# A graph network's first blocks in a new order: block 0 through layer 0 ahead of block 1, its norm on ScalarE, and the setup spread over two passes

## The chip, the cores and the metric

The kernel runs on one core of a Trainium2 chip. A core has five engines that work side by side, each through its own queue in order: TensorE (PE; its weight loads are listed as PEld), VectorE (DVE), ScalarE (ACT), GpSimd (POOL) and SyncE (SP), which here only issues DMA transfers. An engine that meets an instruction whose input isn't there yet waits, and everything behind it in its queue waits too. The metric is the device time of one execution in microseconds; smaller is better.

## The reference

The input x is 128 graphs of 64 nodes with 256 features, and adj is one 64 x 64 adjacency matrix. Four graph layers follow each other, each in the form x = layernorm(x + layer(x)).

```python
# layer 0: attention over adj
Wh = einsum('bnf,fo->bno', x, W)
e = leaky_relu((Wh @ a1)[:, :, None] + (Wh @ a2)[:, None, :], 0.2)
h0 = softmax(where(adj == 0, -inf, e)) @ Wh
# layer 1: attention over 512 edges (src, dst), four heads
e = (leaky_relu(Xq[:, src] + Xq[:, dst], 0.2) * a).sum(-1) + log(adj[src, dst] + 1e-8)
h1 = segment_softmax_and_sum(e, src, Xv[:, dst]) @ W_out.T
# layer 2: (D^-1/2 (adj + I) D^-1/2) x, linear, batchnorm, relu, linear, batchnorm
deg = A.sum(0) + A.sum(1) - diagonal(A)          # A = adj + I
# layer 3: two adjacency layers, then LSTMs over windows of 1, 2, 3 and 4 nodes
```

All of it is float32. Layers 0 and 1 are what the change touches; layers 2 and 3 take most of the time and stay as they are.

## The kernel before

**Blocks.** The 8192 rows of x are cut into 16 blocks (NQ) of 512 rows: 128 partitions by PQ = 4 columns of 256 features, 2 graphs in the partitions of each column. Each block goes through layers 0 and 1 in small steps, which are functions:

- `l0_a` gets the block transposed (block 0 by PE, L231; the others by DVE's transpose of a copy that was loaded in slices, L247). `l0_b` multiplies by W, in which two further columns hold W a1 and W a2 (PE L257, ACT L259), and spreads the second score over 128 columns (`sb`, ACT L262). `l0_c` transposes these (PE L268), adds both scores and the mask (DVE L271), applies the leaky ReLU (L273) and finds the row maximum (L275).
- `l0_x` takes the exponential: for blocks 0 and 1 in four ACT instructions that also sum (L283), for later blocks by a subtraction on DVE (L286) and one ACT instruction (L287). `l0_d` transposes the result on PE (L301) and copies it out on ACT (`eT`, L303). `l0_e` multiplies by the values (PE L311), adds x (DVE L314), and calls `layernorm`: statistics on DVE (L95, L96), the power -1/2 on POOL (L86), and the scaling on POOL (L100). It ends with `load_x(q + 2)`: one DMA for x and eight for the slices, on SP.
- `l1_t` transposes the normed block (PE L231, ACT L232). `l1_qv` makes queries and values for half a block (PE L338 and L341; the queries are split in two by ACT L348 and DVE L349). `l1_graph` forms the edge sums (z, PE L376) and rectifies them (u, ACT L378), `reduce_heads` sums them over features (PE L367). `l1_softmax`, `l1_sums`, `l1_weights` work on two blocks together; `v_a`, `v_b`, `v_c` apply the attention.

**Order.** The program is written down as a list of such calls, and a scheduler puts each engine's instructions in an order of its own, by which input it expects first; the program order of two calls is therefore only a strong hint, and `tc.issue_after` ties an instruction behind another. First comes a head, written out by hand (L580 to L599):

```python
l0_a(0); setup_l0(); ...; l0_b(0); setup_order(); l0_c(0); l0_x(0)
l0_a(1); setup_ends(); l0_b(1); l0_d(0); setup_gather(); setup_queries()
l0_e(0); l0_c(1); l0_x(1); setup_signs(); l0_d(1)
l1_t(0); l1_qv(0, 0); l1_qv(0, 1)
```

Then a loop runs over 16 passes q with eight places b each. At each place one `l1_graph(q, b)` stands, followed by the steps of the list `between[b]`, which belong to blocks q + 1, q + 2 and earlier ones, each tied behind the last PE instruction so far (`step`).

**PSUM.** Nearly all steps take their banks from one ring of three (`bank`, name "m"). A step's first matmul has to wait until the bank's user three places before has been read, by ACT or DVE.

**Setup.** The edges have to be sorted, looked up and counted once. `setup_order`, `setup_ends`, `setup_gather` sort them with comparisons and one-hot matmuls (PE L547, L552; DVE L539 to L559; `gath_r` is what `l1_graph` needs). The rest stands in the list `setup`, from which the loop takes one entry at each place: `setup_zero` (clears two tables by POOL and DMA), `setup_segments` (segment borders, DVE L621 to L624), `setup_bias` (the term log(adj[src, dst] + 1e-8): matmul L655, DVE L657, matmul L659, logarithm on ACT L660), `setup_pairs` (DVE L628 to L634), four times `setup_count` (each three comparisons of 128 x 512 with a sum, DVE L638), `setup_place` (small DVE instructions, L642 to L650) and `setup_adjacency` (degrees of adj + I, scales, and two 128 x 128 matrices for layer 2: DVE L665 to L683, PE L672, L679, L682, POOL L675). Most of these don't depend on the loop, and the scheduler placed many of them into the head: DVE ran L638 from 39 to 50 us.

Of the kernel before, what the change touches and what calls it, by code (L numbers as in the profile page):

```python
# [41 lines left out]
def kernel(ctx: ExitStack, tc: tile.TileContext, i, out):  # L42
# [45 lines left out]
    def layernorm(dst, src, n, engine):  # L88

        st = small.tile([P, n, 6], F32, name="ln_st", bufs=5)  # L90
        mv = small.tile([P, n, 2], F32, name="ln_mv", bufs=5)
        both = small.tile([P, 2, n], F32, name="ln_rs", bufs=5)
        rs, ng = both[:, 0, :], both[:, 1, :]
        for r in range(n):
            nc.vector.bn_stats(st[:, r, :], src[:, r, :])  # L95
            nc.vector.bn_aggr(mv[:, r, :], st[:, r, :])  # L96
        rsqrt(rs, mv[:, :, 1], n)
        nc.vector.tensor_scalar_mul(ng, mv[:, :, 0], -1.0)  # L98
        for r in range(n):
            engine.tensor_scalar(dst[:, r, :], src[:, r, :], ng[:, r:r + 1], rs[:, r:r + 1],  # L100
                                 op0=OP.add, op1=OP.mult)

# [27 lines left out]
    with ExitStack() as two:  # L130
# [147 lines left out]
        def l0_x(q):  # L278
            e, mx = L0[q]["e"], L0[q]["mx"]
            sm = small.tile([P, PQ], F32, name="sm")  # L280
            if q < 2:
                for c in range(PQ):
                    nc.scalar.activation(e[:, c, :], e[:, c, :], AF.Exp, bias=mx[:, c:c + 1],  # L283
                                         accum_out=sm[:, c:c + 1])
            else:
                nc.vector.tensor_add(e, e, mx[:, :, None].to_broadcast([P, PQ, P]))  # L286
                nc.scalar.activation(e, e, AF.Exp)  # L287
            L0[q]["sm"] = sm

        def l0_d(q):  # L290
            e, sm = L0[q]["e"], L0[q]["sm"]
            ri = L0[q]["ri"] = small.tile([P, PQ], F32, name="ri")
            if q < 2:
                nc.vector.reciprocal(ri, sm)
# [10 lines left out]
        def l0_e(q):  # L305
            x, wh, eT, ri = (L0[q][n] for n in ("x", "wh", "eT", "ri"))
            for c2 in range(2):
# [263 lines left out]
        def setup_signs():  # L571
# [4 lines left out]
            for h in range(HEADS):  # L576
                r, c0 = slice((h % 2) * 64, (h % 2 + 1) * 64), CG - HEADS + h
                nc.vector.tensor_copy(apad[r, h // 2, c0:c0 + 1], acol[r, h // 2:h // 2 + 1])

        l0_a(0)  # L580
        setup_l0()
# [15 lines left out]
        l0_d(1)  # L597
        l1_t(0)
        l1_qv(0, 0)  # L599
        l1_qv(0, 1)  # L600


# [48 lines left out]

        def setup_bias():

            pa = bank([E])
            nc.tensor.matmul(pa[:N, :], bd[:N, :N], ohT[:N, 0, :], start=True, stop=True)  # L655
            sel = su.tile([N, E], F32, name="sel")
            nc.vector.tensor_mul(sel, pa[:N, :], ohT[:N, 1, :])  # L657
            pl = bank([E])
            nc.tensor.matmul(pl, ones[:N, :], sel, start=True, stop=True)  # L659
            nc.scalar.activation(lb, pl, AF.Ln, bias=eps8)  # L660

        def setup_adjacency():

            an = su.tile([P, P], F32, name="an")
            nc.vector.tensor_add(an, bd, ident)  # L665
            deg = su.tile([P, 4], F32, name="deg")
# [9 lines left out]
            dd = su.tile([P, P], F32, name="dd")  # L676
            nc.vector.tensor_scalar_mul(dd, ident, deg[:, 3:4])
            ph_ = bank([P])
            nc.tensor.matmul(ph_, an, dd, start=True, stop=True)  # L679
            nc.vector.tensor_scalar_mul(aht, ph_, deg[:, 3:4])  # L680
            pt = bank([P])
            nc.tensor.transpose(pt, bd, ident)  # L682
            nc.vector.tensor_copy(bdT, pt)  # L683
# [22 lines left out]

        def behind(do, q):
            if q < NQ:
                with tc.issue_after([t for t in nc.cur_bb.bb.instructions
                                     if t.engine == mybir.EngineType.Activation][-1]):  # L710
                    do(q)
# [1308 lines left out]
```

## Time and profile before

| what | us |
|---|---|
| median of 3 runs | 2028.21 (2027.94 to 2029.69) |
| the profiled execution, its own time | 2025.54 |
| span of the profiled execution | 2023.8 |
| PE busy in the span | 1934.4 |
| DVE busy | 1277.3 |
| ACT busy | 951.1 |
| POOL busy | 881.1 |
| first matmul | 5.30 |
| first `z` matmul of the loop (L376) | 51.13 |

The page of a profile gives busy time by engine, and the same in 40 slices of 50.6 us as tenths. A row of the timeline gives start, length, engine, line, operation, output and input, the number of instructions merged, and in brackets how long the engine had been idle before it and whose result ended that. In the view of waits a row names the waiting instruction, the one that released it, and the sum, number and longest of these waits in microseconds. The row of windows gives for each stretch of time the busy time of the engines, the TensorE clock that was granted (1.00 is full), and the share of the DMA engines' time in use.

### The profile page before, as it was taken

The page shows a single profiled execution, that of the slowest core. Times are in us where ns is not written, and L with a number is a line of the kernel's source. Part 1 is how long each engine was busy: PE and PEld are TensorE (multiplying, and loading weights), DVE is VectorE, ACT ScalarE, POOL GpSimd, SP SyncE. Part 2 cuts the span into 40 slices and gives each one's busy share as a digit, 9 for nine tenths or more (in the row PEclk, how much of TensorE's full clock was granted, in tenths as well). Part 3 has the DMA queues.
Part 4 walks back from the last instruction along what each step waited for, and adds up shares of the span by engine and source line. Part 5 has one row for each costly group of instructions (what it writes and reads, how often), then busy time and mean ns, then how long its engine had stood idle before and what let it go on. Part 6 is the DMA issues. An engine that isn't in the chain of part 4 may idle for free.

```text
span 2023.8 us, 31384 instructions
## 1 busy us (share of the span) xinstructions
PE 1934.4 (96%) x11447; PEld 1336.6 (66%) x11447; DVE 1277.3 (63%) x2855; ACT 951.1 (47%) x1666; POOL 881.1 (44%) x1020
## 2 busy tenths in 40 slices
PE   5999999998999989899999999999999999999997
PEld 4667777776554445477678577678577668578685
DVE  7567776664556554765566765557865557764566
ACT  2666656665346523644333644343644333543333
POOL 1133343343444632664545544445543445444264
PEclk8999999999999989999999999999999999999998
DMA  5344443332311134432342233133243032131022
GB/s 141 72 68 69 82 79 55 56 56 45 45 46 27 42 132 144 177 125 94 120 141 84 101 124 136 42 130 93 64 146 118 19 115 70 41 120 79 0 63 73
DMA packets 236539, 173.83 MB, mean 86 GB/s; under 512 B 150625, under 2 KB 213601, under 8 KB 233057
## 3 DMA queue, kind: packets, MB, share of 16 engines
q1 hardware_dynamic: 234528, 169.86, 29.6%
q8 instruction: 90, 1.47, 0.3%
q0 software_dynamic: 1024, 1.05, 0.2%
q10 hardware_dynamic: 832, 0.92, 0.1%
q14 instruction: 65, 0.52, 0.1%
HBM read 110.18 MB, written 61.60 MB: 85 GB/s over the span
## 4 chain that ended last, share of the span: by engine, by line
PE 77%; DVE 14%; ACT 4%; issue 2%; POOL 1%; DMA 1%; SPq 0%; DVEq 0%; POOLq 0%; ACTq 0%
PE l L1743 29%; PE l L1699 8%; PE pz L860 4%; PE l L1478 4%; PE m L338 3%; PE pz L789 3%; PE m L257 3%; PE e L367 3%; PE z L376 2%; PE m L461 2%; PE m L341 2%; PE g L1377 2%; PE g L1365 2%; PE pz L1058 2%; DVE cell L1657 1%
## 5 line engine op out<-in xcount | busy, mean ns | idle before, releaser
L1743 PE MATMUL l<-hs,wh 128*128 128x256 f32 (+1 forms) x896 | 276.0, 399 | 3.7 <-DVE hs L1607 3.1
L1743 PE MATMUL l<-xs,wx 128*128 128x256 f32 (+1 forms) x896 | 276.0, 399 | 2.8 <-DVE gate L1762 2.8
L1758 ACT ACTIVATE kept<-l 128x256 f32<-128x256 f32 (+1 forms) x224 | 88.6, 402 | 333.6 <-PE l L1743 332.2
L86 POOL TENSOR_TENSOR ln_rs<-ln_rs,mhalf 128x2 f32<-128x2 f32 (+2 forms) x98 | 85.9, 876 | 344.2 <-DVE ln_rs L98 338.6
L1743 PE MATMUL l<-H,wx 128*128 128x256 f32 (+1 forms) x672 | 210.5, 402 | 4.3 <-DVE gate L1771 3.4
L1743 PE MATMUL l<-hid,wh 128*128 128x256 f32 (+1 forms) x672 | 208.8, 399 | 0.0
L1743 PEld LDWEIGHTS l<-hs,wh 128*128 128x128 f32 x896 | 169.1, 190 | 47.1 <-DVE hs L1607 5.7
L1743 PEld LDWEIGHTS l<-xs,wx 128*128 128x128 f32 x896 | 168.9, 190 | 45.8 <-POOL st L100 2.7
L1699 PE MATMUL l<-H,wx 128*128 128x256 f32 (+5 forms) x672 | 185.0, 431 | 4.9 <-DVE H L116 2.7
L1776 ACT ACTIVATE gate<-gate,bias 128x512 f32<-128x512 f32 (+1 forms) x280 | 170.5, 657 | 40.6 <-DVE gate L1767 34.8
L378 ACT ACTIVATE u<-z 128x1024 f32<-128x1024 f32 x128 | 130.0, 1025 | 71.9 <-PE z L376 71.3
L1699 PEld LDWEIGHTS l<-H,wx 128*128 128x128 f32 x672 | 118.8, 190 | 65.3 <-issue 34.7
L1743 PEld LDWEIGHTS l<-H,wx 128*128 128x128 f32 x672 | 125.7, 190 | 42.6 <-DVE gate L1771 7.4
L1743 PEld LDWEIGHTS l<-hid,wh 128*128 128x128 f32 x672 | 127.2, 190 | 32.0 <-issue 2.9
L1766 POOL TENSOR_TENSOR gate<-gate,kept 128x256 f32<-128x256 f32 (+1 forms) x84 | 65.0, 774 | 145.3 <-DVE kept L1764 145.0
L1771 DVE TENSOR_TENSOR gate<-l,gate 128x256 f32<-128x256 f32 (+1 forms) x112 | 49.9, 446 | 87.6 <-POOL gate L1766 60.8
L349 DVE TENSOR_TENSOR qs<-m,qs 64x256 fp32r<-64x256 f32 x128 | 54.0, 422 | 76.5 <-ACT qs L348 74.4
L1611 POOL TENSOR_TENSOR hs<-hid 128x256 f32<-128x256 f32 (+1 forms) x28 | 26.0, 929 | 171.0 <-DVE hid L1643 87.9
L376 PE MATMUL z<-gath_r,qs 128*128 128x512 f32 x256 | 99.5, 477 | 0.6 <-ACT u L378 0.5
L1665 ACT ACTIVATE gate<-cell 128x512 f32<-128x512 f32 (+1 forms) x88 | 58.6, 666 | 82.6 <-DVE cell L1657 60.6
L1653 POOL TENSOR_TENSOR cell<-gate,cell 128x512 f32<-128x512 f32 (+1 forms) x56 | 75.3, 1366 | 28.2 <-ACT gate L1776 28.2
L1760 DVE TENSOR_TENSOR gate<-l,kept 128x256 f32<-128x256 f32 (+1 forms) x112 | 49.0, 438 | 59.9 <-ACT gate L1776 32.7
(386 smaller groups left out, 4079.4 us busy)
## 6 DMA issues: line engine op xcount, KB each, us to landing
wx<-sums SPq DMA_DIRECT2D x9, 2048.0 KB
wh<-sums SPq DMA_DIRECT2D x9, 1792.0 KB
way<-st SPq DMA_DIRECT2D x54, 256.0 KB
st<-way SPq DMA_DIRECT2D x216, 64.0 KB
xin<-in_x SPq DMA_DIRECT2D x16, 512.0 KB
ld<-table SPq DMA_DIRECT2D x16, 512.0 KB
x_dram<-y SPq DMA_DIRECT2D x16, 512.0 KB
x2r<-x_dram SPq DMA_DIRECT2D x32, 256.0 KB
```

Of the source, the lines that this page charges most:

```text
L86: nc.gpsimd.tensor_tensor(dst, dst, mhalf[:, :n], OP.pow)
L257: nc.tensor.matmul(p_, xT[:, k, c * P:(c + 1) * P], w0[:, k, :], start=k == 0, stop=k == KD - 1)
L376: nc.tensor.matmul(z[:, k, :], L1[q]["qs"][c][:, s, k * P:(k + 1) * P], gath_r, start=True, stop=True)
L378: nc.scalar.activation(u, z, AF.Relu)
L860: nc.tensor.matmul(self.bank[at], lhs, rhs, start=first and n == 0, stop=n == len(self.terms) - 1, skip_group_check=True)
L1478: nc.tensor.matmul(self.bank[at], lhs, rhs, start=new, stop=True, skip_group_check=True)
L1653: nc.gpsimd.tensor_tensor(c, t, c, OP.mult)
L1699: nc.tensor.matmul(b, w.raw[0][:, k, at, m, :], x, start=k == 0, stop=k == KD - 1)
L1743: nc.tensor.matmul(self.banks[j], lhs, rhs, start=src == 0, stop=src == 1)
L1758: nc.scalar.activation(self.keep(j), b, AF.Copy)
L1766: e.tensor_tensor(t[0][:, 1], t[0][:, 1], k[5], OP.add)
L1776: given(lambda: nc.scalar.activation(dst, dst, f, bias=b))
```

## The change

Block 0 goes through the whole of layer 0 before block 1's first matmul, with the lookup's matmul and the logarithm in between. Block 0's norm is scaled by ACT (with one more small DVE product) instead of POOL. Block 1's exponential takes the form of the later blocks, one ACT instruction, and is tied behind ACT's last instruction, after the first half of block 0's queries. Block 1's `l0_e` moves from place (0, 0) of the loop to (0, 1). `setup_adjacency` is cut in three (`setup_degrees`, `setup_scales`, `setup_adjacency`), and the setup list becomes a table of places (q, b); each entry is now tied behind the last PE and the last DVE instruction written before it.

```diff
@@ layernorm
+        if engine is nc.scalar:
+            nc.vector.tensor_mul(ng, ng, rs)
         for r in range(n):
-            engine.tensor_scalar(dst[:, r, :], src[:, r, :], ng[:, r:r + 1], rs[:, r:r + 1],
-                                 op0=OP.add, op1=OP.mult)
+            if engine is nc.scalar:
+                nc.scalar.activation(dst[:, r, :], src[:, r, :], AF.Identity, bias=ng[:, r:r + 1], scale=rs[:, r:r + 1])
+            else:
+                engine.tensor_scalar(dst[:, r, :], src[:, r, :], ng[:, r:r + 1], rs[:, r:r + 1],
+                                     op0=OP.add, op1=OP.mult)
@@ l0_x and l0_d
-            if q < 2:
+            if q == 0:
@@ l0_e
-            layernorm(token_major(q), x, PQ, nc.gpsimd)
+            layernorm(token_major(q), x, PQ, nc.gpsimd if q else nc.scalar)
@@ head
+        def setup_bias():
+            pa = bank([E])
+            nc.tensor.matmul(pa[:N, :], bd[:N, :N], ohT[:N, 0, :], start=True, stop=True)
+            sel = su.tile([N, E], F32, name="sel")
+            nc.vector.tensor_mul(sel, pa[:N, :], ohT[:N, 1, :])
+            around["sel"] = sel
+        def setup_logs():
+            sel = around["sel"]
+            pl = bank([E])
+            nc.tensor.matmul(pl, ones[:N, :], sel, start=True, stop=True)
+            nc.scalar.activation(lb, pl, AF.Ln, bias=eps8)
+        def behind(do, q, engine=mybir.EngineType.Activation):
+            if q < NQ:
+                with tc.issue_after([t for t in nc.cur_bb.bb.instructions if t.engine == engine][-1]):
+                    do(q)
         l0_c(0)
         l0_x(0)
+        setup_ends()
+        setup_gather()
+        setup_bias()
+        l0_d(0)
+        l0_e(0)
+        setup_logs()
         l0_a(1)
-        setup_ends()
         l0_b(1)
-        l0_d(0)
-        setup_gather()
         setup_queries()
-        l0_e(0)
         l0_c(1)
-        l0_x(1)
         setup_signs()
-        l0_d(1)
         l1_t(0)
         l1_qv(0, 0)
+        behind(l0_x, 1)
         l1_qv(0, 1)
+        l0_d(1)
@@ setup
-        def setup_adjacency():
-            an = su.tile([P, P], F32, name="an")
+        def setup_degrees():
+            an = around["an"] = su.tile([P, P], F32, name="an")
             nc.vector.tensor_add(an, bd, ident)
...
+        def setup_scales():
+            an, deg = around["an"], around["deg"]
             pd = bank([P])
             nc.tensor.matmul(pd[:, 0:1], an, ones[:, 0:1], start=True, stop=True)
...
+            pt = bank([P])
+            nc.tensor.transpose(pt, bd, ident)
+            nc.vector.tensor_copy(bdT, pt)
+        def setup_adjacency():
+            an, dd, deg = (around[n] for n in ("an", "dd", "deg"))
             ph_ = bank([P])
             nc.tensor.matmul(ph_, an, dd, start=True, stop=True)
             nc.vector.tensor_scalar_mul(aht, ph_, deg[:, 3:4])
-        setup = [setup_zero, setup_segments, setup_bias, setup_pairs]
-        setup += [lambda c=c: setup_count(c) for c in range(EC)]
-        setup += [setup_place, setup_adjacency]
+        counts = [lambda c=c: setup_count(c) for c in range(EC)]
+        setup = {(0, 0): [setup_zero], (0, 1): [setup_segments], (0, 2): [setup_degrees, setup_pairs], (0, 3): [setup_scales],
+                 (1, 1): counts[:1], (1, 2): counts[1:3] + [setup_adjacency], (1, 3): counts[3:] + [setup_place]}
@@ loop
-                [(l0_e, q + 1), (l0_a, q + 2)],
-                [(sums, q if q else -1), (l1_softmax, S)],
+                [(l0_e, q + 1 if q else -1), (l0_a, q + 2)],
+                [(l0_e, -1 if q else 1), (sums, q if q else -1), (l1_softmax, S)],
...
-                if setup:
-                    setup.pop(0)()
+                for do in setup.get((q, b), ()):
+                    step(lambda _: behind(lambda _: do(), 0, mybir.EngineType.DVE), 0)
```

More of the change, by code (lines that the diff above doesn't have):

```diff
@@ L292, in l0_d @@
             ri = L0[q]["ri"] = small.tile([P, PQ], F32, name="ri")
-            if q < 2:
+            if q == 0:
                 nc.vector.reciprocal(ri, sm)
@@ L578, in setup_signs @@
                 nc.vector.tensor_copy(apad[r, h // 2, c0:c0 + 1], acol[r, h // 2:h // 2 + 1])
+        around = {}
+        def setup_bias():
[13 more added lines that the diff above has]
+                    do(q)
         l0_a(0)
@@ L650, in setup_place @@
             nc.vector.tensor_copy(place, at_f[:, :, 1])
[L652 to L660, printed above, removed]
-        def setup_adjacency():
-            an = su.tile([P, P], F32, name="an")
+        def setup_degrees():
+            an = around["an"] = su.tile([P, P], F32, name="an")
             nc.vector.tensor_add(an, bd, ident)
-            deg = su.tile([P, 4], F32, name="deg")
+            deg = around["deg"] = su.tile([P, 4], F32, name="deg")
             nc.vector.reduce_sum(deg[:, 0:1], an, axis=AX.X)
@@ L675, in setup_adjacency @@
             nc.gpsimd.tensor_tensor(deg[:, 3:4], deg[:, 2:3], mhalf[:, 0:1], OP.pow)
-            dd = su.tile([P, P], F32, name="dd")
+            dd = around["dd"] = su.tile([P, P], F32, name="dd")
             nc.vector.tensor_scalar_mul(dd, ident, deg[:, 3:4])
+            pt = bank([P])
[3 more added lines that the diff above has]
+            an, dd, deg = (around[n] for n in ("an", "dd", "deg"))
             ph_ = bank([P])
@@ L680, in setup_adjacency @@
             nc.vector.tensor_scalar_mul(aht, ph_, deg[:, 3:4])
-            pt = bank([P])
-            nc.tensor.transpose(pt, bd, ident)
-            nc.vector.tensor_copy(bdT, pt)
-        setup = [setup_zero, setup_segments, setup_bias, setup_pairs]
-        setup += [lambda c=c: setup_count(c) for c in range(EC)]
-        setup += [setup_place, setup_adjacency]
+        counts = [lambda c=c: setup_count(c) for c in range(EC)]
+        setup = {(0, 0): [setup_zero], (0, 1): [setup_segments], (0, 2): [setup_degrees, setup_pairs], (0, 3): [setup_scales],
+                 (1, 1): counts[:1], (1, 2): counts[1:3] + [setup_adjacency], (1, 3): counts[3:] + [setup_place]}
         LAG = BPS + 1
@@ L705, in step @@
             queue.extend(mine[-1:])
[L707 to L711, printed above, removed]
         def sums(q):
```

## The prediction

> **What bounds the kernel now.** I read the page first, then PE's waits over the first 110 us, PE's queue in order of time, the windows, and last the queues of DVE, ACT and SP over the same stretch. Line numbers are those of the kernel before; "period q" is the pass over block q, counted from one l0_e matmul group (L311) to the next.
>
> ```profile
> span 2023.8 us, 31384 instructions
> PE 1934.4 (96%) x11447; PEld 1336.6 (66%) x11447; DVE 1277.3 (63%) x2855; ACT 951.1 (47%) x1666; POOL 881.1 (44%) x1020
> ...
> PE   5999999998999989899999999999999999999997
> ```
>
> PE is the bound: 96% busy, at 9 tenths nearly everywhere. The first slice (50.6 us) has 5. What the change touches is all there and in the next two slices, so the question is how many microseconds PE loses there and whether later stages keep what is won; PE leads the chain everywhere behind (77% of it), so I let a head start pass through unshortened. The waits of PE from 10 to 110 us (us in total, times, longest):
>
> ```profile
> PE m L301 <- ACT e L283: 6.2, 1, 6.2
> ...
> PE m L301 <- ACT e L287: 2.8, 2, 2.1
> PE m L338 <- DVE A L648: 2.6, 1, 2.6
> PE m L257 <- DVE ri L294: 2.3, 1, 2.3
> PE m L268 <- ACT lb L660: 1.5, 1, 1.5
> PE m L679 <- DVE A L677: 1.3, 1, 1.3
> PE m L311 <- ACT A L303: 1.2, 1, 1.2
> ```
>
> That is 17.9 us of standing. PE's queue shows where, and that block 1's projection (L257, at 24.29) stands ahead of block 0's attention (L301, L311):
>
> ```profile
> 24.29 5.44 PE L257 MATMUL m<-w,tT 128*128 128x258 f32 x16 [2.33 <-DVE ri L294]
> 29.56 0.60 PE L301 MATMUL m<-ident,e 128*128 128x128 f32 x4
> 31.34 1.99 PE L311 MATMUL m<-A 128*128 128x256 f32 x8 [1.18 <-ACT A L303]
> ...
> 50.37 1.11 PE L338 MATMUL m<-wq,tT 128*128 128x260 f32 x4 [2.62 <-DVE A L648]
> ...
> 56.53 2.15 PE L311 MATMUL m<-wh,eT 128*128 128x256 f32 x8
> ...
> 59.45 3.65 PE L257 MATMUL m<-w,tT 128*128 128x258 f32 x16
> ```
>
> The same sixteen passes L257 take 5.44 us at 24 and 3.65 at 59. In windows of 2 us the granted clock (the third number from the end) says why:
>
> ```profile
> 24.00:26.00 2.00, 1.71 (x5) 1.41 (x6) 2.00 (x8) 0.03 (x1) 0.00 (x0) 0.68 0.42 149
> 26.00:28.00 2.00, 2.00 (x6) 1.53 (x6) 1.88 (x12) 0.65 (x2) 0.00 (x0) 0.50 0.00 0
> ```
>
> After each gap of 1.9 us or more (at 22, 34, 48, 76 and 131 us) some 3.5 us ran at 0.50, which costs 1.7 us each; after the gaps of 1.5 us and less there was none. **A rule weighed:** the Trainium skill ("TensorE: Matmul & The Clock Gate", What's actually happening) has half clock only after an idle window of about 3.4 us. By it four of those five gaps would have cost nothing more, and the gap of 2.3 us that I find in the head below would be free, and the sum 13.2 instead of 11.5. I take the row: a gap above 1.9 us costs itself and 1.7.
>
> The windows of periods 0 and 1 (length, then busy us of PE, PEld, DVE, ACT, POOL; clock; DMA) show how much room DVE, the third number, has for what is moved there, 14.7 and 11.1 us:
>
> ```profile
> 56.50:84.60 28.10, 24.53 (x110) 16.96 (x109) 13.37 (x37) 19.41 (x31) 3.18 (x5) 0.94 0.31 48
> 84.60:109.40 24.80, 22.82 (x127) 16.38 (x126) 13.66 (x42) 15.86 (x28) 3.69 (x6) 1.00 0.34 59
> ```
>
> **Head, to block 1's L311 (before: 56.53).** The changed program, as built, orders PE's queue L547, L552, bias matmul (L655), L301(0), L311(0), logarithm's matmul (L659), L257(1), L268(1), L231(0), the queries. Until 18.3 us nothing differs. Then, with the trace's durations:
> - DVE no longer does L665 and L667 there (0.5 us): L271(0) at 18.3, row maxima at 21.8, exponentials 21.9 to 23.5 on ACT.
> - PE: L552 ends at 21.4; L655 needs the one-hot rows (L558, done 22.5): 22.5 to 23.6 (1.07); L301(0) to 24.2 (0.60); eT on ACT (0.60) to 24.8; L311(0) at 24.9, against 31.34. DVE's product of L655 (0.68, L657) ends at 24.9 too and frees the second bank of L311.
> - DVE: residual L314 starts 1.17 after L311 and ends 2.9 after it, 27.8; statistics, 1.9, to 29.7; POOL's power (L86, 1.04) to 30.7; the new product ng*rs, a tiny DVE one (L98's 0.16), 30.9. POOL's clear of the table (2.02) fits before, 27.0 to 29.0.
> - PE meanwhile: L659 26.9 to 28.0 (1.12), L257(1) to 31.65 at full clock. ACT loads the logarithm's table (1.28) while L311 runs and takes the logarithm (0.69) at 28.0: no engine waits.
> - The norm on ACT: four ACTIVATEs 128x256. Nearest rows: 0.38 (64x256) and 0.63 (128x512), so 0.4 each, 31.0 to 32.6, against 3.21 on POOL (L100). Behind it on ACT stand two wh copies and sb: 33.9; PE's L268(1) waits for that, a gap of 2.3 us.
> - L268(1) and L231(0) to 35.4; tT copies to 36.1. DVE's scores of block 1 (1.1 and three of 0.7) run 34.6 to 37.7, so the differences (L349) start at 37.7; queries 0 to 39.3, three z, queries 1 from 40.1 to 43.6 (3.5 each, L338 and L341); the exponential's table load and exp stand on ACT between the two. L301(1) at 44.7 (bank), eT at 46.4: L311(1) at 46.4.
>
> 56.53 - 46.4 = 10.1; for the gap of 2.3 us one half-clock stretch, 1.7: **8.4 won.** As a check: gaps and half clock between 17.5 and 56.5 before come to 12.5 + 5.8 (1.7 at L257, 2.4 at 40, 1.7 at 52) = 18.3; after keep 6.1 of gaps, 1.7 of half clock, and hold 2.7 more work (L655, L659, two z).
>
> **Period 0.** Segments, pairs, degrees and scales (about 5.3 us of DVE) come after block 1's statistics, where DVE was idle 4.7 and 2.3 us. L311(1) to L268(2): before 12.25. After: the two bias matmuls and the logarithm's load are gone, but the degrees' matmul waits for DVE, and its bank, needed by L231(1), comes free behind the pairs, 9.8 after L311: 10.35, **1.9 won.** L268 to L301: 9.68 before, with the exponential's load ahead (76.48). That load is now in the head: **1.3 won**, and the wait of 2.09 falls to 0.8, so its half clock goes too: L301 to L311, 6.12, becomes 4.4, **1.7 won**. **A rule weighed:** "ScalarE: Activation LUTs" (What ACT_TABLE_LOAD costs) adds a drain of 1.38 us to the load's 1.28. In the trace a copy ends at 76.48, the load starts at 76.48 and exp at 77.77: I take 1.28; by the page 1.4 more would be won here (12.9 in all), less what the same drain cost behind the head's loads.
>
> **Period 1 (before: 24.81).** Here the counts land: 12 x 0.79 (L638 with its read, start to start) = 9.5 us of DVE, and aht and place, 1.0, between block 2's statistics (done 5.3 after L311) and block 3's scores (L271), which ran 12.8 after L311. DVE's idle time there was 7.3. So scores start at 15.5 and end at 19.2, 3 late. Also aht (L680) stands behind nine counts, at 12.7, and holds the bank that L268(3) needs at 10.2: a gap of 2.5. L349 is behind the scores, ACT's queries behind L349, the exponential behind those: L301 at 22.15, next L311 at 26.6. The adjacency's wait of 1.3 is gone and counted. **1.8 lost**; the half clock after the gap falls into time in which PE would wait for DVE. Bounds: 0 (the counts fit into the idle time) and 5.3 (a second gap of 1.8 and the 1.7 behind it).
>
> At no cost: the seg memset (idle DVE before and after), POOL (44% busy; one norm fewer), DMA issues. SP: block 2's x stands behind ACT's norm instead of POOL's, with weights and table clears behind it, all earlier. Six of block 3's eight slices now wait behind its x, for POOL's norm of block 1: issued by 59, needed at about 69 by DVE's transpose (L247); the same slices, an x and both tables took 12 us before (41 to 53). If this cover failed DVE would stand, and L349 and PE with it.
>
> **Sum.** 8.4 + 1.9 + 1.3 + 1.7 - 1.8 = 11.5. The profiled execution took 2025.54 (span 2023.8, 1.7 around it); the median is 2.7 above it: 2028.2 - 11.5 = **2016.7**.
>
> **The rivals.**
> - More won (0.14): PE stays warm through the head (1.7) and the counts fit (1.8), and period 2's stall at 131 us (1.9 and 1.8) shifts away: 18.7, 2009.5. For it: the counts sit in DVE's longest idle stretch. Against: the in-order bank behind them.
> - Less won (0.14): half clock in both L311(0) to L257(1) and the queries (3.4 more) and period 1 at its upper bound (3.5 more): 4.6 won, 2023.6. For it: L552's two-column matmuls before 21.4 load PE little, and the clock fell after them before.
> - No difference (0.09): block 3's six late slices reach DVE's transpose 10 us after it could start, DVE stands for that time and PE with it: 1.5 won, 2026.7. Against: they would have to take 20 us, where eight slices, an x and the tables took 12.
> - **Slower (0.07): DVE becomes the bound of periods 0 and 1.** The setup's 4.6 us net in period 0 and 10.5 in period 1 lie in the open, because PE's banks come free only by DVE's queue, and they leave three half-clock stretches (5.1). 20.2 lost against 13.3 won: 7 us slower, 2035. It decides from 13.3 us of exposed DVE on. Against: DVE was busy 13.4 of 28.1 us in period 0 and 13.7 of 24.8 in period 1.
>
> **Numbers.** My forecast 0.56, the rivals 0.14, 0.14, 0.09, 0.07. Faster 0.84 (the first three), same 0.09, slower 0.07; 0.2% (4 us) is about what a measurement here tells from nothing. Range 2010 to 2023.7: from nearly all of "more" to "less".
>
> **What would show it.** Right: block 0's L311 near 25 us, block 1's near 47, PE's wait of 6.2 us for ACT's exponentials gone, the exponential's table load before 45, period 0 near 23 us, period 1 near 26.6 with PE's L268 waiting for aht. Wrong: a period 1 above 30, a stop of DVE at L247 for a DMA, an L231(0) later than 38, or the head start shrinking after 140 us.

## The result and the profile after

On one chip the changed kernel takes 2018.6 us (median, 2017.13 to 2019.22) and the kernel before 2029.18 us (2027.94 to 2030.43): ratio 0.9955, interval [0.9943, 0.9968]. That is 9.1 us less by the ratio (the medians differ by 10.6); the spans of the two profiled executions differ by 8.4.

Lines of the changed kernel stand 5 higher in this part: L316 is the l0_e matmul (L311 of before), L262 the projection (L257), L273 and L276 the score's transposes and sums (L268, L271), L236 the transposes of l1_t (L231), L306 those of the exponentials (L301). L666 are the counts (L638), L707 is aht (L680), L693 the degrees' matmul, L706 that of the adjacency.

The page:

```profile
span 2015.4 us, 31385 instructions
...
PE 1932.2 (96%) x11447; PEld 1334.4 (66%) x11447; DVE 1279.8 (64%) x2858; ACT 952.3 (47%) x1663; POOL 878.7 (44%) x1016
...
PE   6899999998999989899999999999999999999996
```

The first slice went from 5 to 6, the second from 9 to 8. PE's busy time fell by 2.2 us (it was 1934.4) with the same 11447 instructions, while its granted clock over the span went from 0.986 to 0.988; the other 6.2 of the 8.4 us are idle time removed. Some of that was given back in the second slice. The waits of PE from 10 to 110 us:

```profile
...
PE m L273 <- ACT sb L267: 2.1, 1, 2.1
PE m L273 <- DVE aht L707: 1.7, 1, 1.7
PE m L306 <- ACT e L292: 1.5, 2, 0.8
...
PE m L236 <- ACT tT L237: 1.2, 1, 1.2
...
PE m L693 <- DVE A L683: 1.0, 1, 1.0
```

The wait of 6.2 for block 1's exponentials is gone. PE's queue in order of time shows what stands in its place:

```profile
25.51 3.46 PE L316 MATMUL m<-A 128*128 128x256 f32 x8 [0.69 <-ACT A L308]
...
36.43 0.66 PE L273 MATMUL m<-ident,sb 128*128 128x128 f32 x4 [2.10 <-ACT sb L267]
...
49.14 3.20 PE L316 MATMUL m<-wh,eT 128*128 128x256 f32 x8 [0.53 <-ACT eT L308]
...
73.94 1.89 PE L316 MATMUL m<-wh,eT 128*128 128x256 f32 x8
...
86.45 0.63 PE L273 MATMUL m<-ident,sb 128*128 128x128 f32 x4 [1.69 <-DVE aht L707]
...
96.45 0.66 PE L306 MATMUL m<-ident,e 128*128 128x128 f32 x4 [0.81 <-ACT e L292]
```

The same eight matmuls L316 take 3.46, 3.20 and 1.89: the first two groups ran mostly at half clock. The starts of L316 (L311), block by block, serve as markers from here on:

| block | before | after | ahead by |
|---|---|---|---|
| 0 | 31.3 | 25.5 | 5.8 |
| 1 | 56.5 | 49.1 | 7.4 |
| 2 | 84.6 | 73.9 | 10.6 |
| 3 | 109.4 | 100.9 | 8.5 |
| 4 | 139.2 | 130.5 | 8.7 |
| 15 | 458.4 | 449.9 | 8.6 |

The head start is made by block 2, partly lost in period 1, and then carried to the end (8.4 in the span). These are one trace each; in a second trace of the changed kernel ("again" in the next table) it is 6.5 ahead at block 2 and 5.5 at block 3.

### The profile page after: what moved, and what is told of

It reads as the page before. It is cut to its first block, busy times and chain, and to the rows that moved or that the text cites. A ratio compares the mean times of both kernels' runs of the same rounds, so it can differ in the third digit from the quotient of the medians.

```text
span 2015.4 us, 31385 instructions
## 1 busy us (share of the span) xinstructions
PE 1932.2 (96%) x11447; PEld 1334.4 (66%) x11447; DVE 1279.8 (64%) x2858; ACT 952.3 (47%) x1663; POOL 878.7 (44%) x1016
## 4 chain that ended last, share of the span: by engine, by line
PE 75%; DVE 15%; ACT 3%; issue 2%; POOL 2%; DMA 2%; SPq 0%; DVEq 0%; POOLq 0%; ACTq 0%
PE l L1761 27%; PE l L1717 8%; PE pz L878 4%; PE l L1496 4%; PE m L343 3%; PE pz L807 3%; PE e L372 3%; PE z L381 2%; PE m L466 2%; PE m L346 2%; PE m L262 2%; PE g L1395 2%; PE g L1383 2%; PE pz L1076 2%; PE m L316 1%
## 5 line engine op out<-in xcount | busy, mean ns | idle before, releaser
L1671 POOL TENSOR_TENSOR cell<-gate,cell 128x512 f32<-128x512 f32 (+1 forms) x56 | 75.3, 1366 | 28.1 <-ACT gate L1794 28.1
L1778 DVE TENSOR_TENSOR gate<-l,kept 128x256 f32<-128x256 f32 (+1 forms) x112 | 49.1, 438 | 60.1 <-ACT gate L1794 32.7
```

The costliest lines, as they stand in the source:

```text
L1671: nc.gpsimd.tensor_tensor(c, t, c, OP.mult)
```

## The experiments

Ratios are to the kernel before on the same chip, with 95% intervals. Where a ratio can't separate two kernels, the markers of one profiled execution each are the evidence; how far those repeat is shown by the changed kernel run again. "Period 0" runs from block 1's L316 to block 2's, "period 1" on to block 3's.

| kernel | ratio | block 1 | block 2 | block 3 | period 0, 1 |
|---|---|---|---|---|---|
| changed kernel | 0.9955 [0.9943, 0.9968] | 49.1 | 73.9 | 100.9 | 24.8, 27.0 |
| setup only | 0.997 [0.9958, 0.9982] | 49.8 | 77.5 | 103.2 | 27.7, 25.8 |
| head only | 0.9996 [0.9989, 1.0002] | 51.6 | 75.3 | 105.6 | 23.7, 30.3 |
| norm on POOL | 0.9948 [0.9934, 0.9961] | 50.2 | 76.1 | 103.0 | 25.9, 26.9 |
| logarithm in the loop | 0.9965 [0.9951, 0.9978] | 49.1 | 79.6 | 105.4 | 30.5, 25.8 |
| no counts | 0.9947 [0.9933, 0.9961] | 51.3 | 78.3 | 101.2 | 27.0, 22.8 |
| aht first | 0.9957 [0.9943, 0.9971] | 51.0 | 78.0 | 103.8 | 27.0, 25.8 |
| counts late | 0.9985 [0.9978, 0.9992] | 50.9 | 75.8 | 99.7 | 24.9, 23.9 |
| fillers | 0.9959 [0.9945, 0.9973] | 49.3 | 74.0 | 99.7 | 24.7, 25.8 |
| room | 0.9954 [0.9939, 0.997] | 47.2 | 69.7 | 98.5 | 22.5, 28.8 |
| room and fillers | 0.9951 [0.9939, 0.9964] | 46.5 | 69.0 | 97.7 | 22.4, 28.8 |
| changed kernel again | 0.9967 [0.9955, 0.9978] | 51.1 | 78.1 | 103.9 | 27.0, 25.8 |
| spread | 0.9926 [0.9913, 0.9939] | 47.6 | 70.1 | 93.8 | 22.5, 23.7 |

**Half of the change each.** Setup only: the new table of places in the old head. Head only: the new head with the old list.

```diff
 # setup only, in the kernel before
-        setup = [setup_zero, setup_segments, setup_bias, setup_pairs]
...
+        setup = {(0, 0): [setup_zero], (0, 1): [setup_segments], (0, 2): [setup_bias, setup_degrees, setup_pairs], (0, 3): [setup_scales],
+                 (1, 1): counts[:1], (1, 2): counts[1:3] + [setup_adjacency], (1, 3): counts[3:] + [setup_place]}
 # head only, in the changed kernel
-                for do in setup.get((q, b), ()):
-                    step(lambda _: behind(lambda _: do(), 0, mybir.EngineType.DVE), 0)
+                if setup:
+                    setup.pop(0)()
...
+        setup = [setup_zero, setup_segments, lambda: None, setup_pairs]
+        setup += [lambda c=c: setup_count(c) for c in range(EC)]
+        setup += [setup_place, all_adjacency]
```

> The kernel before with one part of the change: the setup's entries in the slots of the changed kernel (counts in period 1), the head in its old order, the logarithm still in the loop. By the sum: the counts leave the head, so PE's wait of 2.6 us at 48 us and the half clock behind it (1.7) go, and about 1.5 of DVE's work ahead of block 1's exponential; block 1's l0_e matmuls near 51 instead of 56.5. Period 0 stays near 28 (both table loads are still in it), period 1 grows from 24.8 to about 27. Net 3 to 4 us faster than before. Rival (the slots are the whole gain): 8 to 9 us. Rival (the order is the whole gain): within 1 us of before.

> The changed kernel with the other part alone: its head, its norm and its logarithm, but the setup as the old list, tied to nothing, so that the counts go back into the head. By the sum: block 0's l0_e near 26; DVE's counts then stand ahead of block 1's scores and between its query differences, so block 1's l0_e comes near 53 instead of 49; period 1 is back at 24 to 25 instead of 27. Net 6 to 8 us faster than before. Rival (the slots are the whole gain): within 1 us of before. Rival (the order is the whole gain): 8 to 9 us faster, as the changed kernel.

Measured: the setup alone is worth about 6 us by its ratio (0.997 of 2024; the interval allows 3.6 to 8.5) and is 6.2 ahead at block 3, more than forecast. It brings block 1 to 49.8, within 0.6 of the changed kernel's first trace, although PE's wait for block 1's exponentials is still there, 5.25 long instead of 6.20:

```profile
38.71 0.86 PE L301 MATMUL m<-ident,e 128*128 128x128 f32 x2 [5.25 <-ACT e L283]
```

Its interval overlaps those of both measurements of the changed kernel, so the ratios don't exclude that the places of the setup are the whole gain. The head alone is worth at most 2.2 by its interval, though it is 9.3 ahead at block 2. Where it loses them stands in PE's queue of the head-only kernel:

```profile
75.33 1.89 PE L316 MATMUL m<-wh,eT 128*128 128x256 f32 x8
85.39 0.79 PE L706 MATMUL m<-A 128*128 128x128 f32 x2 [4.91 <-DVE A L698]
```

The adjacency in one piece puts a matmul on PE behind a product on DVE (L698). What that product waits for stands in the queues of DVE (first row) and POOL (the other two):

```profile
85.05 0.28 DVE L698 TENSOR_SCALAR A<-ident,A 128x128 f32<-128x128 f32 x1 [3.77 <-POOL A L696]
82.34 2.16 POOL L105 TENSOR_SCALAR A<-xin,ln_rs 128x256 f32<-128x256 f32 x4
84.46 0.55 POOL L696 TENSOR_TENSOR A<-A,mhalf 128x1 f32<-128x1 f32 x1
```

The degrees' power (L696) stood on POOL behind block 2's norm, and PE stopped for 4.9; in the changed kernel this power ran in period 0, at 61.04. This points to the cut of `setup_adjacency` in three as what lets the new head keep its gain; no run here makes that cut alone. The two halves don't add up (at block 2, 7.1 and 9.3 ahead alone; together 10.6 in one trace and 6.5 in the other), presumably because both empty the same stretch of the head.

**The norm on ScalarE.** Block 0's norm is put back on POOL.

```diff
-            layernorm(token_major(q), x, PQ, nc.gpsimd if q else nc.scalar)
+            layernorm(token_major(q), x, PQ, nc.gpsimd)
```

> The changed kernel with block 0's norm scaled by POOL again. If the norm's engine is on the path: POOL takes 2.2 to 3.2 us instead of ACT's 2.07, the queries start up to 1.2 later, and the time is 1 us up. If what holds PE at 34 to 36 us are the two wh copies and sb that stand behind the norm on ACT: they come 2 us earlier, the score transposes start near 34.3 instead of 36.4, block 1's scores on DVE 2 us earlier, and the queries start at about 38 as now: no difference, or up to 0.5 us faster.

Measured: no worse (the intervals overlap). From block 0's L316 to block 1's L273 it took 9.8 us, against 10.9 with the norm on ACT; PE's gap before L273 is 1.14 against 2.10. To block 1's L316 it took 22.6, against 23.6 in both traces of the changed kernel. ACT's queue in the changed kernel says why:

```profile
33.10 2.07 ACT L103 ACTIVATE A<-xin,ln_rs 128x256 f32<-128x256 f32 x4 [0.29 <-DVE ln_rs L100]
35.08 0.63 ACT L264 ACTIVATE wh<-m 128x258 f32<-128x258 f32 x2
35.75 0.63 ACT L267 ACTIVATE sb<-wh 128x512 f32<-128x512 f32 x1
```

The four scalings take 0.52 each, and block 1's second wh copies and sb, for which PE waits, stand behind them. This part of the change costs about 1 us in its stretch; that is below what the ratios can tell.

**The logarithm back in period 0.** It moves from the head to place (0, 2).

```diff
-        setup_logs()
...
-        setup = {(0, 0): [setup_zero], (0, 1): [setup_segments], (0, 2): [setup_degrees, setup_pairs],
+        setup = {(0, 0): [setup_zero], (0, 1): [setup_segments], (0, 2): [setup_logs, setup_degrees, setup_pairs],
```

> The changed kernel with the logarithm and its matmul back in the loop (period 0, third place), all else as changed. By the sum both table loads are in period 0 again: period 0 grows by the matmul (1.1) and about 2.6 of ACT, from 24.8 to 27 or 28.5; block 1's l0_e comes up to 1.5 earlier than 49.1. Net 1 to 3 us slower than the changed kernel. Rival (ACT has room for the loads in the loop): within 0.5 us of it.

Measured: period 0 is 30.5; it is 24.8 and 27.0 in the two traces of the changed kernel. Compare it with the second: in both, two cells in a row at half clock fell on the middle of the period (59.8 to 66.6 here, 61.2 to 68.0 there). ACT's queue in that period:

```profile
56.17 1.28 ACT L599 ACT_TABLE_LOAD   x1
71.57 1.28 ACT L292 ACT_TABLE_LOAD   x1
```

and PE's behind the second load:

```profile
73.55 1.12 PE L306 MATMUL m<-ident,e 128*128 128x128 f32 x4 [2.09 <-ACT e L292]
```

Both table loads are back, and PE waits 2.09 for the exponential, as it did before; a stretch at half clock follows, and from L306 to L316 it takes 6.1 instead of 4.4. The load itself stays 1.28: no row shows the further drain that the Trainium skill ("ScalarE: Activation LUTs", What ACT_TABLE_LOAD costs) adds. The ratios don't separate this kernel from the changed one (0.9965; 0.9955 and 0.9967), so the gain in the period, about 3.5 us with 1.6 of it clock, rests on the markers alone.

**The counts.** Three kernels: the counts are left out (their sums set to zero; the sorting's places are then not those of the edges); aht is moved ahead of them, to place (1, 0), so that its bank comes free early; and, with aht there, half of them are moved to places (1, 5) and (1, 7).

```diff
 # no counts
-            for n in range(3):
-                nc.vector.tensor_scalar(less, pair_r, pair[:, c, n:n + 1], 0.0, op0=OP.is_lt, op1=OP.add,
-                                        accum_out=below3[:, c, n:n + 1])
+            if c == 0:
+                nc.vector.memset(below3, 0.0)
 # aht first
-                 (1, 1): counts[:1], (1, 2): counts[1:3] + [setup_adjacency], (1, 3): counts[3:] + [setup_place]}
+                 (1, 0): [setup_adjacency], (1, 1): counts[:1], (1, 2): counts[1:3], (1, 3): counts[3:] + [setup_place]}
 # counts late
+                 (1, 0): [setup_adjacency], (1, 1): counts[:1], (1, 2): counts[1:2], (1, 5): counts[2:3], (1, 7): counts[3:] + [setup_place]}
```

> The changed kernel without its twelve comparisons (the counts that weight the edges are set to zero instead; all else stays). If DVE's 9.5 us of counts are what makes period 1 longer: its l0_e to l0_e falls from 27.0 to about 23, PE's wait of 1.7 us for aht and the half clock behind it are gone, periods 0 and 2 stay (24.8, 29.6), and the time is 3 to 4 us below the changed kernel. If the counts were hidden in DVE's idle time and period 1 is longer for another reason: period 1 stays at 26 to 27 and the time within 1 us.

> The changed kernel with setup_adjacency at the first place of period 1, ahead of all counts, so that its PSUM bank comes free early. If the bank behind nine counts is what PE loses by in period 1: the wait of 1.7 us is gone, with it the half clock (1.7), period 1 falls from 27.0 to about 24, and the time by 2 to 3 us. If DVE's queue as a whole is late (the scores stand behind all counts): PE waits the same time one step later, for the scores' bank or the exponential, and period 1 stays within 1 us of 27.

> The changed kernel with the adjacency first and the counts spread: six of the twelve comparisons ahead of block 3's scores, three between the queries' differences, three at the end of period 1. If it is the backlog on DVE ahead of the scores: scores start 4 us earlier, period 1 falls from 27.0 to 24 or 25; the three last comparisons move into period 2 ahead of the residual, which may give 1 us back there. Time 1 to 3 us below the changed kernel. If any added DVE work costs PE its own length (DVE is the bound): period 1 and 2 together stay at 56.6 and the time as now.

Without counts period 1 is 22.8, against 25.8 where no half clock fell into it (fillers, and the changed kernel again) and 27.0 where it did: the counts cost 2.9, with the half clock 4.1. (Its period 0 caught more half clock than the first trace of the changed kernel, so block 3 is no earlier, and the ratio doesn't show it.) With aht first, PE's wait of 1.69 is gone and period 1 is still 25.8, as in the changed kernel's second trace, which has that wait. The time comes back in two places of the same period:

```profile
94.18 1.15 PE L343 MATMUL m<-wq,tT 128*128 128x260 f32 x4 [0.50 <-DVE e L276]
99.36 0.66 PE L306 MATMUL m<-ident,e 128*128 128x128 f32 x4 [2.25 <-ACT e L292]
```

So the held bank was not the bound; DVE's queue ahead of block 3's scores was. With half of the counts later, period 1 is 23.9, but period 2 is 33.1 instead of 28.1, and the time is worse. The rows of period 2:

```profile
111.99 0.33 PE L236 MATMUL m<-ident,A 128*128 128x128 f32 x1 [2.11 <-POOL A L105]
113.50 0.47 PE L236 MATMUL m<-ident,A 128*128 128x128 f32 x1 [1.18 <-POOL A L105]
114.93 1.86 PE L236 MATMUL m<-ident,A 128*128 128x128 f32 x6 [0.96 <-POOL A L105]
```

The late counts now delay the next block's statistics on DVE, POOL's norm waits for those and PE for POOL; the last six transposes, 1.86, also ran into half clock. Moved there, the cost was not saved.

**Filler matmuls.** Two groups of 128x512 matmuls that nothing reads, in PE's gaps at 22 and 25 us.

```diff
+        def warm(n):
+            z = bank([KD, E], name="z", bufs=2)
+            with tc.issue_after([t for t in nc.cur_bb.bb.instructions if t.engine == mybir.EngineType.PE][-1]):
+                for _ in range(n):
+                    nc.tensor.matmul(z[:, 0, :], ident, iota_e, start=True, stop=True)
         setup_bias()
+        warm(1)
         l0_d(0)
+        warm(1)
         l0_e(0)
```

> The changed kernel with two more float32 matmuls of 128x512 (0.86 us each at full clock, into a bank that nobody reads) in PE's gaps at 22 and 25 us. If the clock falls after cells of 3.41 us in which PE was busy for less than about half: no half clock falls on block 0's l0_e, which takes 2.0 us instead of 3.5; from there to block 1's l0_e 23.6 becomes 22 or so, and the time falls by 0.5 to 1.7 us in spite of more work. If the half clock has another cause: l0_e stays at 3.5 us and the time goes up by up to 0.5.

Measured: block 0's L316 took 1.98 instead of 3.46, so the half clock there did come from the gaps before it (in "room" below, fillers take it from 3.62 to 1.98). But 36 to 39 then ran at half clock and block 1's L316 still started at 49.3: a stretch was moved, not removed.

**Other places for the setup.** "Room" gives the setup's buffers storage of their own, so that degrees, scales and pairs can run at the end of block 1's projection in the head, and one count in the head's last stretch; the rest of the counts stand singly, and block 0's norm is on POOL.

```diff
+        behind(lambda _: setup_degrees(), 0, mybir.EngineType.DVE)   # after l0_b(1)
+        behind(lambda _: setup_scales(), 0, mybir.EngineType.DVE)
+        behind(lambda _: setup_pairs(), 0, mybir.EngineType.DVE)
...
+        behind(lambda _: setup_count(0), 0, mybir.EngineType.DVE)    # after l1_qv(0, 0)
...
+        setup = {(0, 0): [setup_zero], (0, 1): [setup_segments], (0, 3): counts[1:2], (1, 0): [setup_adjacency],
+                 (1, 1): counts[2:3], (1, 2): counts[3:4], (1, 3): [setup_place]}
```

> The setup's DVE work in another place: degrees, scales and pairs at the end of DVE's work on block 1's projection in the head, one of four counts (three instructions) in the head's last stretch, one in period 0, two ahead of block 3's scores at most, the last with place; the norm of block 0 back on POOL. If DVE's queue ahead of a block's scores is what makes periods 0 and 1 long (counts measured 3 to 4 us in period 1, the degrees' chain waits of 1.0 and 1.2 in period 0), then: block 1's l0_e at 49 to 50, period 0 22 to 24, period 1 23.5 to 25, block 3's l0_e near 96 to 98 instead of 100.9, and a time 3 to 5 us below the changed kernel (2013 to 2016, ratio to before about 0.993). Rival, the counts and the degrees cost PE the same wherever they stand on DVE: block 3's l0_e stays within 1 us of 100.9, ratio near 0.9955. Second rival, the head loses it: pairs and degrees ahead of block 1's scores move block 1's l0_e to 51 or later.

> The same with two filler matmuls of 512 columns in PE's gaps at 22 and 25 us. If a stretch at half clock follows any 3.4 us cell of the clock's grid in which PE was busy for about half or less, block 0's l0_e matmuls take 2.0 instead of 3.4 and what follows starts 1 to 1.5 earlier; whether that is kept to block 1's l0_e depends on where the later cells fall: 0 to 1.5 us below the kernel without them. Rival, the fillers only take up PE and the banks: same or slower by up to 0.7.

> The changed kernel as it is, beside the others on the same chip. Ratio 0.995 to 0.996 (9 us). If the clock's cells lie at another phase in each execution, the lengths of the head and of the periods differ from those of its first trace (49.1, 24.8, 27.0) by up to 1.7 each, with the waits themselves unchanged: the wait for aht at 1.5 to 2, the wait for sb near 2. If the lengths are the schedule's alone they repeat to 0.3.

Room won the head and period 0 (block 2 at 69.7, 4.3 ahead of the changed kernel) and lost it again in period 1, much as the head-only kernel had: I had put the product for the adjacency (here L706) into the entry at (1, 0), behind block 2's statistics on DVE.

```profile
75.54 0.49 PE L708 MATMUL m<-A 128*128 128x128 f32 x2 [4.00 <-DVE A L706]
```

The fillers make no difference that the ratios show. The changed kernel again gave 0.9967, and its executions ran from 2013.46 to 2024.29. Its waits for aht (1.7) and sb (2.3) repeat, that for the degrees (L693) doesn't (2.1 instead of 1.0), nor do its periods: 27.0 and 25.8, where the first trace has 24.8 and 27.0. So markers of single traces are good to about 2 us in each period.

**Spread.** Room, with that product in period 0 and the matmul one place later:

```diff
+        def setup_spread():
+            nc.vector.tensor_scalar_mul(around["dd"], ident, around["deg"][:, 3:4])
...
-            nc.vector.tensor_scalar_mul(dd, ident, deg[:, 3:4])
...
-        setup = {(0, 0): [setup_zero], (0, 1): [setup_segments], (0, 3): counts[1:2], (1, 0): [setup_adjacency],
-                 (1, 1): counts[2:3], (1, 2): counts[3:4], (1, 3): [setup_place]}
+        setup = {(0, 0): [setup_zero], (0, 1): [setup_segments, setup_spread], (0, 3): counts[1:2],
+                 (1, 1): [setup_adjacency] + counts[2:3], (1, 2): counts[3:4], (1, 3): [setup_place]}
```

> The room kernel of before showed block 1's l0_e at 47.2, period 0 of 22.5, and then a stop of 4.0 of PE in period 1: the matmul of the adjacency stood on PE behind a product on DVE (dd) that stood behind all of block 2's statistics. Here that product stands behind the segments in period 0, and the matmul one place later. If the stop was that order alone, block 1's l0_e stays at 47 to 48, period 0 at 22.5 to 23, the wait for dd is gone, period 1 is 24 to 25.5 instead of 28.8 (the counts and place still end at about 11.8 behind l0_e, some 2 after the scores could start), and block 3's l0_e is at 94 to 96, 5 to 7 ahead of the changed kernel; time 3 to 6 below the changed kernel, ratio to before 0.992 to 0.994. Rival, DVE's eight counts and place ahead of block 3's scores only show up as the next wait: period 1 of 27 or more, and the ratio stays at 0.995.

Ratio 0.9926 [0.9913, 0.9939], about 15 us below before and below both intervals of the changed kernel: the fastest version, median 2013.26. Like room it has block 0's norm on POOL. PE's row for the adjacency has no wait:

```profile
74.22 0.49 PE L710 MATMUL m<-A 128*128 128x128 f32 x2
```

and DVE reaches the scores of block 3 just as they are ready:

```profile
81.84 1.13 DVE L276 SCALAR_TENSOR_TENSOR e<-m,wh,mask 128x128 f32<-128x128 f32 x4 [0.16 <-PE m L273]
```

In the changed kernel twelve comparisons and aht stand between the statistics and that point; here six do, with aht and place, and it is DVE that waits, 0.16. Period 1 is 23.7, 0.9 above the kernel without counts. Both its periods ran at full clock. What half clock added to period 0 of the changed kernel I estimate from its rows: in the second trace 0.5 in the transposes L236 and 2.3 between L273 and L306 (10.5 instead of 8.2), which leaves 24.2 of the 27.0; in the first 0.6 (see the next section), which leaves 24.2 of the 24.8. Against 24.2 and the 25.8 of period 1 the order itself wins about 1.7 and 2.1. The rest of the markers' difference is the head (22.0 from block 0 to block 1 instead of 23.6; the norm on POOL alone had won 1.1 of this) and the clock. Of the 7.1 that it is ahead at block 3, its profiled execution shows only 2.6 in the span (2012.8). The windows from 440 to 520 us have most of the rest in the granted clock (third number from the end), 0.98 in the changed kernel:

```profile
440.00:520.00 80.00, 73.13 (x752) 47.62 (x753) 44.62 (x106) 40.05 (x61) 30.28 (x34) 0.98 0.22 43
```

and 0.91 in this one:

```profile
440.00:520.00 80.00, 73.35 (x660) 45.86 (x660) 42.07 (x98) 36.34 (x55) 27.82 (x32) 0.91 0.21 36
```

0.07 of 80 us are some 5 us of lost clock in that one execution; its other executions went down to 2007.04.

## Why the prediction was right, and where its terms were off

The forecast was 11.5 won; the two traces show 8.5 won at block 3 and 8.4 in the span, and the ratios of the two measurements give 9.1 and 6.7. The direction held, and the waits that the forecast named went or came where it had them. Three terms were too favourable; in the last two the clock has a part. What the forecast did not ask is which half of the change wins the head: by the setup-only kernel, most of it comes from the counts leaving it. That the order adds to this is not shown: the ratios can't tell, and the markers of the two traces disagree (at block 2 10.6 and 6.5 ahead, with the setup alone 7.1).

**Head: 8.4 forecast, 7.4 measured.** Block 0's L316 started at 25.5 (24.9 forecast), PE's wait for sb was 2.10 (2.3), the exponential's table load stood at 43.01, and nothing waited for it. The logarithm's load did not run ahead while L316 ran, as I had it; it stood behind its matmul, and PE waited 0.18 for the logarithm. The 1.0 less is 0.8 up to L273, 0.5 from there to L306, and 0.3 the other way behind it. Of the 0.8, 0.6 is there before the change begins to act: block 0's projection, the same sixteen matmuls, took 6.09 instead of 5.52 (6.64 in the second trace). One half-clock stretch of 1.7 was in the sum, and one came, but at 26 to 29 and not behind the gap of 2.1 us; that the count was right is luck. The forecast's own check gives 18.3 - 6.1 - 1.7 - 2.7 = 7.8, nearer to what came, and I passed over the difference; and its sign "block 1's near 47" left out the 1.7 of its own sum, which puts it at 48.1.

**Period 0: 4.9 forecast, 3.2 measured.** This is the term that missed most. From L273 on it was right: L306 began 8.2 after L273 (9.68 - 1.3 = 8.4 forecast), and L316 4.4 after L306 (4.4). But from block 1's L316 to L273 it took 12.15 instead of 10.35. A half-clock stretch that the sum did not have lies in there: L316(1) took 3.20, though by my rule no gap of the last stretch of the head was long enough for one (1.27 and 0.53). It is not the main cause. In the second trace L316(1) took 1.99, at full clock, and L273 still came 12.04 behind it. PE's wait for the degrees, in the first trace (first row) and in the second (the others):

```profile
58.21 0.35 PE L693 MATMUL m<-A 128*128 128x1 f32 x2 [1.00 <-DVE A L683]
...
59.64 0.35 PE L693 MATMUL m<-A 128*128 128x1 f32 x2 [2.13 <-DVE A L683]
...
62.23 1.12 PE L236 MATMUL m<-ident,A 128*128 128x128 f32 x4 [1.17 <-ACT tT L237]
63.14 1.06 PE L273 MATMUL m<-ident,sb 128*128 128x128 f32 x4
```

The degrees' first sum (L683) stands on DVE behind block 1's statistics and the segments; a PE that comes earlier waits longer for it. The last four transposes L236, for which I had 9.8 behind L316, began at 11.7 and 11.1. These L236 took 0.5 longer than the 0.66 of the first trace, by half clock; without it L273 would have come some 11.5 behind L316. So of the 1.8 about 1.2 is the queue, mis-sized, and 0.6 the clock.

**Period 1: 1.8 lost forecast, 2.1 measured.** The aht wait was named, and was 1.69 instead of 2.5; the scores began 14.75 after L316 (15.5 forecast), L306 22.5 (22.15), the next L316 27.0 (26.6). In DVE's queue:

```profile
85.96 0.35 DVE L707 TENSOR_SCALAR aht<-m,A 128x128 f32<-128x128 f32 x1
...
88.69 0.35 DVE L276 SCALAR_TENSOR_TENSOR e<-m,wh,mask 128x128 f32<-128x128 f32 x1
```

What was wrong is where I let the half clock behind the aht wait fall "into time in which PE would wait for DVE". The fillers kernel and the second trace have the same wait of 1.69 without the half clock, and their period 1 is 25.8: the stretch cost 1.2.

**The rule for the clock.** "A gap above 1.9 us costs itself and 1.7" was wrong in its form, and its price is a ceiling: a stretch cost 1.6 in the head (22.0 from block 0 to block 1 in room, 20.4 with the fillers), 1.2 in period 1 and about 0.6 in period 0, where PE would have waited anyway. Cut into cells of 3.41 us, both traces have every half-clock stretch of these periods filling whole cells of one grid. The grid's rows of before, a cell and the next (length; busy us of PE and the others; the granted clock is the third number from the end):

```profile
75.92:79.33 3.41, 1.32 (x8) 0.86 (x8) 1.42 (x4) 3.39 (x5) 0.00 (x0) 1.00 0.02 5
79.33:82.74 3.41, 3.41 (x10) 2.70 (x9) 1.01 (x4) 2.01 (x4) 0.00 (x0) 0.50 0.00 0
```

and of after, its three stretches, and the gap for sb that cost none:

```profile
22.52:25.93 3.41, 2.08 (x8) 1.01 (x9) 3.34 (x8) 2.11 (x9) 0.00 (x0) 0.99 0.01 2
25.93:29.34 3.41, 3.41 (x9) 2.29 (x8) 1.67 (x7) 0.00 (x0) 0.26 (x1) 0.51 0.00 0
...
32.76:36.17 3.41, 1.57 (x8) 1.02 (x6) 0.16 (x1) 3.09 (x8) 0.11 (x1) 1.00 0.00 0
36.17:39.58 3.41, 2.90 (x18) 2.53 (x19) 2.32 (x6) 1.29 (x3) 0.00 (x0) 1.00 0.87 245
...
46.41:49.82 3.41, 1.60 (x9) 1.21 (x9) 2.85 (x7) 2.94 (x6) 0.00 (x0) 0.99 0.94 355
49.82:53.23 3.41, 3.41 (x10) 2.69 (x9) 2.88 (x9) 0.18 (x1) 0.00 (x0) 0.51 0.11 22
...
83.96:87.37 3.41, 1.68 (x11) 1.22 (x11) 3.30 (x10) 2.22 (x4) 0.00 (x0) 0.99 0.51 160
87.37:90.78 3.41, 3.41 (x17) 0.60 (x16) 3.34 (x16) 1.02 (x1) 0.00 (x0) 0.51 1.14 144
```

Between 18 and 140 us these two traces have nine cells in which PE was busy for at most 1.68 us, about half; eight of them were followed by a cell at half clock, however the idle time was cut into gaps: 1.27 and 0.53 at 46 to 50 were enough. Only two cells with more (1.81 and 2.08) were. So where a gap falls on the grid matters. The wait for sb was 2.28 in the fillers kernel and 2.27 in the second trace of the changed kernel; in the first it lies in one cell (the first two rows), in the second across two (the last two):

```profile
32.93:36.34 3.41, 1.13 (x11) 1.14 (x11) 0.37 (x2) 2.19 (x7) 0.00 (x0) 1.00 0.18 50
36.34:39.75 3.41, 3.41 (x11) 2.45 (x10) 2.83 (x6) 1.19 (x2) 0.00 (x0) 0.50 1.11 290
...
33.87:37.28 3.41, 2.06 (x9) 1.44 (x8) 0.16 (x1) 2.95 (x8) 0.95 (x1) 1.00 0.00 0
37.28:40.69 3.41, 2.06 (x14) 1.78 (x15) 1.51 (x5) 2.10 (x5) 0.00 (x0) 1.00 0.56 172
```

A sharp threshold is not shown. The cell with 1.57 above was followed by full clock, as was one with 1.50 (at 122.9) in the kernel without counts; the first with 2.08 was followed by half (narrow and 64-row matmuls are in it; whether those count less wasn't tried).

**The rivals.** "Slower, DVE becomes the bound" did not come: DVE was busy 18.6 of 24.8 us in period 0 and 22.0 of 27.0 in period 1, and period 1 grew by 2.1. A part of it was there, though: the counts cost 3 to 4 us of PE's time, of their 9.5 on DVE. "No difference", DVE stopped at the transposes by late slices, did not come either: DVE's row for block 3's transpose (74.10) shows no idle time ahead of it. "Less won" came in part: 3.0 of its 6.9 us were lost at block 3 in the first trace, and 6.0 in the second.

## What to carry to other kernels

One-off work fits into an engine's idle share only if no in-order queue puts it between a block's data and the bottleneck's next instruction: the counts in one row cost 3 to 4 us in their period; with half of them in earlier places that period was 0.9 longer than without any. A product of 0.25 us in the wrong place stopped PE for 4.0, a power of 0.55 us for 4.9. Where an instruction of the bottleneck depends on a small one of another engine, write the small one a full stage earlier. And try each half of a change alone: here the setup's places alone gave 0.997, the head alone 0.9996, and the whole 0.9955 and 0.9967.

## What the hardware showed that I had not expected

The half clock sits on a grid of 3.41 us whose place differs from execution to execution (a stretch began at 25.9 in one trace of the changed kernel and at 23.6 in the other, which is not a multiple of 3.41 apart). The Trainium skill ("TensorE: Matmul & The Clock Gate", What's actually happening) has such a free-running window, and the grid agrees with it; that the window before has to be idle doesn't: cells with 1.08 to 1.68 us of matmuls were followed by 0.50. The thirteen executions of the changed kernel's second measurement spread by 10.8 us, and their granted clock goes along: 0.991 in the two fastest (2013.46 and 2014.08), 0.984 in the slowest (2024.29). That the grid's place makes this spread is argued from this, not shown.
